# Four PSUM banks for the scan during the 5x5 convolution of images 1 to 3

## The chip, the cores and the metric

The kernel runs on one core of one Trainium2 chip. The metric is the device time of one execution in microseconds, a median over runs. The core has five engines with a queue each: TensorE (PE, with its weight loads as PEld), VectorE (DVE), ScalarE (ACT), GpSimd (POOL) and SyncE (SP, which issues DMAs here). PSUM, where matmuls put their results, is used in eight banks of 128 x 512 fp32.

## The reference, cut to what matters

Four layers, each pre-normed and residual, on `x` of 4 images, 128 channels, 64 x 64 pixels, all fp32:

```python
x = x + attention(_gn(x))          # 4096 pixels attend to each other, per image
x = x + conv5x5(_gn(x))            # radial 128 -> 128 kernel, padding 2
x = x + scan_layer(_gn(x))         # Wx, two directions of a state-space scan, Wp
x = x + conv3x3(_gn(x))            # main_w, main_b; the offset branch selects out or out
```

`_gn` is a group norm with 32 groups of four channels. In the scan layer each direction has 64 channels and 64 states: for every channel and state the recurrence is `h[t] = exp(delta[t] * A) * h[t-1] + delta[t] * x[t] * B[t]` over the 4096 pixels, and `y[t]` is the sum over states of `h[t] * C[t]`, plus `D * x[t]`.

## The kernel before

**The scan and its ticks.** `scan_core` cuts one image's scan into 256 ticks (`TICKS`), 1024 in all. A tick is a chunk of 1024 pixels (`CH`), a direction, a group of four states (`q`, 16 of them) and one of two channel groups of 32 (`g`), so that 128 partitions hold 32 channels by four states. Its steps lie on different engines:

- `drive(i)` (L1250): GpSimd, `db = dx * B`, 128 x 1024, three buffers.
- `decay(i, h)` (L1235): ScalarE, `da = exp(a * delta)`, written to PSUM. With two banks free for a tick it is done in two halves of 512, from three one-bank buffers of the pool `s2`. With the pool `wide` it is one instruction of 1024 over two banks, from two two-bank buffers.
- `recur(i)` (L1255): VectorE, the scan itself (L1263), in halves or whole, and where `to_pool(i)` is false also the product with C (L1266).
- `weigh(i)` (L1281): GpSimd, the product with C where `to_pool(i)` is true (L1284).
- `keep(i)` (L1271): ScalarE, saves the last column for the next chunk (L1279).
- `collect(i)` (L1286): TensorE, sums states into the bank `y` by small matmuls (L1304), for four ticks at a time. The tiles `hc` between the products and these matmuls have eight buffers.

`to_pool` (L1197) gives GpSimd two of every five products as a rule, three of five while `"operands"` is in `ready`, one of five while `"drives"` is, and one of three in the last image.

**The rest of the work.** Everything else is written as generators that yield the estimated cost of what they issued. `images()` (L1481) does image 0 up to its scan operands, then for each further image attention, `conv_pairs` (the 5x5 convolution), `scan_prep` and `scan_operands`, and at last the back parts (output projection and 3x3 convolution). `program` (L1376) walks the ticks: in each half of a tick it adds half of `pace` to a credit (2.8 us a tick, 1.5 for the last image) and takes steps from `images()` until the credit is used. So while the scan of image b-1 runs, attention and convolution of image b are laid between its ticks, and the order on every engine is that of the issue. `before(b)` (L1537) draws all steps that are missing until the first operands of image b are ready, four ticks ahead of its first tick.

**Around the change.** At the end of `attention` (L663) `settle` issues the last block and puts `(b, "attended")` in `ready`. `conv_pairs` (L828) begins with memsets on GpSimd, the group norm (13 small VectorE instructions, and two on GpSimd, L381 and L382), and four `normalise` pieces on ScalarE (L387). Then it does four chunks of matmuls (L962), which use the banks `s`, `a` and `z`. For images 1 to 3 it is `lean`: the first sum `q` is added by one more matmul (L989), and VectorE adds the result to the image (L930) with a running sum for the next norm. After the last addition `(b, "convolved")` is set and `scan_prep` (L1001) issues memsets and the next group norm. Attention uses the bank `s2` for scores; `scan_operands` uses it as one of three for the matmuls of L1044 and L1079. `conv_pairs` doesn't.

**The banks.** Four banks (`s`, `a`, `z`, `y`) are always there. The other four are the pool `s2` (one bank of that tag, three of `da`) or the pool `wide` (two `da` tiles of two banks). `widen` (L1503) swaps to `wide` once, when all operands of the last image are issued. At a swap the loop does `recur(i)` and `keep(i)` first, closes the old pool, opens the new, and only then issues the next `decay`.

Of the kernel before, what the change touches and what calls it, by code (L numbers as in the profile page):

```python
# [29 lines left out]
PSUM = bass.MemoryType.PSUM  # L30
# [15 lines left out]
PRODUCT, HOP, SLOT, PACE, ENDPACE, AHEAD = 0.86, 1.7, 0.7, 2.8, 1.5, 4  # L46
# [6 lines left out]
def conv_preact_kernel(  # L53
# [17 lines left out]
    B, C, H, W = x.shape  # L71
# [19 lines left out]
    pools, ready = {}, set()  # L91
# [345 lines left out]
    def attention(b, xs, xn, v, st, safe, loads):  # L437
# [141 lines left out]
        def settle(blk):  # L579
            raw, pb = state.pop(blk)  # L580
            cut = bass.ts(blk, MM)
            nc.vector.tensor_tensor(pb, raw, pb, ALU.mult)
            nc.vector.scalar_tensor_tensor(  # L583
                xs[:, cut], pb, bv_c, xs[:, cut], ALU.add, ALU.add, accum_out=st.sum(blk)
            )
            st.squares(blk, xs[:, cut], xs[:, 0:1])
# [75 lines left out]
        yield PRODUCT  # L662
        settle(blk)  # L663
        ready.add((b, "attended"))


    def conv(b, xs, tag, st, weights, k, finish, name, residual=False):
# [147 lines left out]
    def more_weights(cw, to):  # L815

        w = [cw[:, n * 5 : (n + 1) * 5, :] for n in range(3)]
        half, dif = to[:, 0], to[:, 1]
        nc.vector.tensor_tensor(half, w[0], w[2], ALU.add)
        yield HOP  # L820
        nc.vector.tensor_scalar(half, half, 0.5, None, ALU.mult)
        yield HOP
        nc.vector.scalar_tensor_tensor(dif, w[1], -0.5, half, ALU.mult, ALU.add)
        yield HOP
        nc.vector.scalar_tensor_tensor(half, w[1], 0.5, half, ALU.mult, ALU.add)
        yield HOP

    def conv_pairs(b, xs, tag, st, st2, lean):  # L828
# [36 lines left out]
        wide = pools.get("fill") if not lean else None  # L865
# [70 lines left out]
        for c in range(L // CH):  # L936
# [20 lines left out]
            for n, (acc, parts) in enumerate(accs):  # L957
# [13 lines left out]
                if n == 0:  # L971
                    qs = pools["bg"].tile([P, MM], F32, tag="w", bufs=4, name=f"q_{b}_{c}")

                    def done(acc=acc, qs=qs, c=c):
                        nc.scalar.copy(qs, acc)
                        for y in range(0 if lean else 2):
                            nc.gpsimd.tensor_tensor(
                                chunk(xs, c, y), chunk(xs, c, y), flat(qs), ALU.add
                            )
# [14 lines left out]
        yield HOP  # L994
        done()
        ready.add((b, "convolved"))

# [185 lines left out]
    def scan_core(mats4, ynds, before, widen, result):  # L1185


        ticks = [
            (b, c, d, q, g) for b in range(B)
            for c in range(NCH) for d in range(2) for q in range(NQ) for g in range(KG)  # L1190
        ]
# [5 lines left out]
        def to_pool(i):  # L1197


            if i not in pooled:  # L1200
                n = i % 5
                pooled[i] = (
                    i % 3 == 2 if ticks[i][0] + 1 == B
                    else n == 1 if "drives" in ready
                    else n % 2 == 0 if "operands" in ready else n % 2 == 1
                )
            return pooled[i]
# [73 lines left out]
        def weigh(i):  # L1281
            b, c, d, q, g = ticks[i]
            if to_pool(i):
                nc.gpsimd.tensor_tensor(hcs[i], hcs[i], rows["c", b, c, d, q], ALU.mult)  # L1284
# [49 lines left out]
        n = len(ticks)  # L1334

        def do(step, i, *args):
            if 0 <= i < n:
                step(i, *args)

        for i in range(-AHEAD, n + 4):  # L1340
            if (i + AHEAD) % TICKS == 0 and i + AHEAD < n:
                before((i + AHEAD) // TICKS)
            do(drive, i + 2)
            do(keep, i - 1)
            late = widen is not None and i + 1 < n and ticks[i][0] == B - 1 and widen()
            if not late:
                do(decay, i + 1, 0)
            do(recur, i)
            if late:
                do(keep, i)  # L1350
                late()
                widen = None
                do(decay, i + 1, 0)
            do(weigh, i - 1)
            do(collect, i - 3)
            yield i
            do(decay, i + 1, 1)
            do(load, i + AHEAD)
            yield i
# [16 lines left out]
    def program(safe):  # L1376
# [65 lines left out]
        def end(b, pieces):  # L1442

            xs, st, yt = ends[b]
            yield from scan_end(b, xs, st, yt, pieces)
# [35 lines left out]
        def images():  # L1481
            begun = yield from start(0)
            for b in range(B):
                begun = yield from front(b, *begun)
            for a in range(B - 1):
                yield from stage(a, range(NM), "scan")
                yield from end(a, range(NM))
                yield from back(a)
            for pieces, done in ((inner, "inner"), (last, "last")):
                yield from stage(B - 1, pieces, done)  # L1490
                yield from end(B - 1, pieces)
            yield from stage(B - 1, range(PER), "lower")
            ready.add((B - 1, "staged"))

        with ExitStack() as es, tc.manual_schedule():
            if safe:
                pools["big"] = es.enter_context(tc.tile_pool(name="big_safe", bufs=1))
                pools["bg"] = es.enter_context(tc.tile_pool(name="bg_safe", bufs=2))
            banks = ExitStack()
            pools["s2"] = banks.enter_context(tc.tile_pool(name=f"narrow{safe}", bufs=1, space=PSUM))  # L1500
            pools.pop("wide", None)

            def widen():  # L1503

                def swap():
                    banks.close()
                    pools["wide"] = es.enter_context(
                        tc.tile_pool(name=f"wide{safe}", bufs=1, space=PSUM)
                    )
                    del pools["s2"]  # L1510

                return swap if (B - 1, "all") in ready else None

            work = images()
            if not safe:
                with tc.tile_pool(name="fill", bufs=2) as pools["fill"]:
                    while not (0, "begun") in ready:
                        next(work)
                    more = [
                        pools["fill"].tile([P, NTAP, C], F32, tag="taps", bufs=1, name="taps"),  # L1520
                        pools["fill"].tile([P, 2, 5, C], F32, tag="more", bufs=1, name="more"),
                    ]

                    with tc.tile_pool(name="tables", bufs=1) as tmp:
                        for _ in chain(scan_constants(), build_conv_weights(tmp, more[0]), more_weights(*more)):
                            for _ in range(4):
                                next(work)
                    while (0, "convolved") not in ready:
                        next(work)
                del pools["fill"]  # L1530
                setup.close()
            pools["rep"] = es.enter_context(tc.tile_pool(name=f"rep{safe}", bufs=3))
            pools["rows"] = es.enter_context(tc.tile_pool(name=f"rows{safe}", bufs=3))
            pools["hc"] = es.enter_context(tc.tile_pool(name=f"hc{safe}", bufs=8))
            pace = PACE

            def before(b):  # L1537

                nonlocal pace
                while (b, "operands", 0) not in ready:  # L1540
                    next(work)
                if b + 1 == B:
                    pace = ENDPACE

            def result():

                while (B - 1, "staged") not in ready:
                    next(work)
                return ends[B - 1][2]

            credit = 0.0
            for i in scan_core(mats4, ynds, before, widen, result):
                if i % TICKS == 6 and i > TICKS:
                    ready.add((i // TICKS - 1, "scan"))
                if i == B * TICKS - TICKS // NCH + 6:
                    ready.update({(B - 1, "inner"), (B - 1, "lower")})
                if i == B * TICKS - TICKS // NCH // 2 + 6:
                    ready.add((B - 1, "last"))
                credit = min(credit + pace / 2, pace)
                while credit > 0:  # L1560
                    credit -= next(work, pace)
            for _ in work:
                pass
            for _ in chain(end(B - 1, range(PER)), back(B - 1)):
                pass

    program(False)
    lower.close()

# [12 lines left out]
    with tc.If(again > 0):  # L1582
        program(True)
# [59 lines left out]
```

## Time and profile before

| | |
|---|---|
| time, median of 3 runs | 4448.21 us (4447.31 to 4449.51) |
| the profiled execution | 4449.83 us |
| its span, first to last instruction | 4448.0 us |
| TensorE busy | 3922.3 us, 88% |
| VectorE busy | 3722.6 us, 84% |
| GpSimd busy | 3637.1 us, 82% |
| ScalarE busy | 2398.0 us, 54% |
| granted TensorE clock, mean | 0.936 |
| first tick of images 0, 1, 2, 3 | 695.3, 1648.7, 2595.6, 3537.1 us |
| 5x5 convolution of images 1, 2, 3 on TensorE | from 1384.9, 2328.2, 3272.7 to 1560.5, 2506.3, 3448.2 us |
| first unparted tick | tick 772, at 3568.7 us |

Shares over the whole span mix stages: image 0 runs without a scan, three images run with all engines shared, and the last image's scan has the back parts beside it. Busy times of TensorE are from modelled ends, so starts are the better measure there. A group line gives line, engine, operation, output and inputs with shapes, count, busy us, mean ns, and after the bar the idle time of the engine just before and what ended it. A line of the timeline gives start, length, engine, line, operation and, in brackets, idle time before it with its releaser. A line by stretch gives for each engine its busy us and instructions, then the granted clock, the share of the DMA engines and GB/s.

### The profile page before, as it was taken

Reading aid. Unit: us, or ns where it says so; the run is one execution under the profiler, and the core shown is the slowest. Engines: PE = TensorE matmul, PEld = TensorE weight load, DVE = VectorE, ACT = ScalarE, POOL = GpSimd, SP = SyncE. Lnnn points to the kernel's source line nnn. Section 1 sums busy time; section 2 is a strip of 40 time slices with the busy share of each in tenths; the row PEclk is TensorE's granted clock in tenths of the full one; section 3 lists DMA queues with packets and bytes.
Section 4 is the critical chain, followed back from the end, with each engine's and each line's share of the span. In section 5 each row is a group of like instructions: output and inputs, shape, how many; then the busy total and the mean of one; then the engine's idle time right before and its main releaser. Section 6 shows DMA issues by size and latency. Waiting matters only on the chain. (4 is left out here: it accounts for less than half of the span.)

```text
span 4448.0 us, 43613 instructions
## 1 busy us (share of the span) xinstructions
PE 3922.3 (88%) x13480; PEld 1492.0 (34%) x13480; DVE 3722.6 (84%) x3703; ACT 2398.0 (54%) x4425; POOL 3637.1 (82%) x1728
## 2 busy tenths in 40 slices
PE   8999997999999979999999889999999657576666
PEld 4444433333333323333333333333333112121222
DVE  4722217999999978999999889999999899999995
ACT  3333226666665476666664576666654754444532
POOL 3433307999999978999999889999999899999995
PEclk9999999999999989999999989999999869787887
DMA  1000016545545565455545565455445666656562
GB/s 64 21 1 1 0 55 230 182 163 178 178 173 177 178 228 195 173 178 173 182 167 173 205 228 178 166 178 179 169 178 178 225 217 208 229 199 232 189 228 78
DMA packets 213171, 726.10 MB, mean 163 GB/s; under 512 B 25152, under 2 KB 26432, under 8 KB 212672
## 3 DMA queue, kind: packets, MB, share of 16 engines
q1 hardware_dynamic: 211328, 722.49, 46.0%
q8 instruction: 108, 1.77, 0.2%
q14 instruction: 135, 1.11, 0.1%
q10 hardware_dynamic: 1600, 0.73, 0.1%
HBM read 653.98 MB, written 69.14 MB: 163 GB/s over the span
## 5 line engine op out<-in xcount | busy, mean ns | idle before, releaser
L1253 POOL TENSOR_TENSOR db<-dx,br 128x1024 f32<-128x1024 f32 x1024 | 2398.3, 2365 | 219.5 <-DMA dx<-dxd 59.5
L1246 ACT ACTIVATE da<-de,a_neg 128x512 f32<-128x512 f32 (+1 forms) x1796 | 1343.9, 751 | 741.7 <-DVE da L1263 435.5
L482 PE MATMUL sc<-r,x 128*128 128x512 f32 x2048 | 1080.8, 610 | 11.1 <-ACT last L1279 5.2
L494 PE MATMUL acc<-exchange,v 128*128 128x512 f32 x2048 | 1050.2, 595 | 2.2
L1284 POOL TENSOR_TENSOR hc<-hc,cr 128x1024 f32<-128x1024 f32 x401 | 947.9, 2364 | 17.8 <-ACT last L1279 15.3
L1266 DVE TENSOR_TENSOR hc<-da,cr 128x512 f32<-128x512 f32 (+1 forms) x1078 | 835.5, 775 | 66.8 <-DVE da L1263 0.5
L488 ACT ACTIVATE exchange<-sc 128x512 f32<-128x512 f32 x1024 | 603.2, 589 | 513.6 <-PE sc L482 508.3
L1304 PE MATMUL y<-hc,sel 128*32 128x512 f32 x4096 | 606.4, 647 | 261.6 <-POOL hc L1284 248.7
L1263 DVE TENSOR_TENSOR_SCAN da<-da,last,db 128x512 f32<-128x512 f32 (+1 forms) x464 | 728.3, 1570 | 17.2 <-POOL db L1253 14.7
L1263 DVE TENSOR_TENSOR_SCAN da<-da,da,db 128x512 f32<-128x512 f32 x455 | 585.5, 1287 | 14.9 <-ACT da L1246 14.4
L482 PEld LDWEIGHTS sc<-r,x 128*128 128x128 f32 x2048 | 363.1, 190 | 579.7 <-issue 383.8
L494 PEld LDWEIGHTS acc<-exchange,v 128*128 128x128 f32 x2048 | 387.2, 190 | 499.5 <-issue 479.3
L1263 DVE TENSOR_TENSOR_SCAN hc<-da,last,db 128x512 f32<-128x512 f32 (+1 forms) x304 | 455.7, 1499 | 2.3 <-POOL db L1253 0.7
L1263 DVE TENSOR_TENSOR_SCAN hc<-da,hc,db 128x512 f32<-128x512 f32 x317 | 406.7, 1283 | 43.5 <-ACT da L1246 13.8
L536 POOL TENSOR_TENSOR sidep<-sidep,exchange 128x512 f32<-128x512 f32 x120 | 170.9, 1424 | 273.3 <-ACT exchange L488 271.0
L1304 PEld LDWEIGHTS y<-hc,sel 128*32 128x32 f32 x4096 | 114.6, 112 | 692.4 <-POOL hc L1284 342.1
L536 DVE TENSOR_TENSOR sided<-sided,exchange 128x512 f32<-128x512 f32 x120 | 95.9, 799 | 221.5 <-ACT exchange L488 220.1
L1263 DVE TENSOR_TENSOR_SCAN da<-da,db 128x512 f32<-128x512 f32 (+1 forms) x159 | 235.8, 1483 | 11.3 <-ACT da L1246 7.3
L696 PE MATMUL pcm<-xpm,cs 128*128 128x512 f32 x432 | 211.7, 639 | 35.8 <-ACT xpm L387 35.8
L516 PE MATMUL zp<-exchange,ones 128*32 128x512 f32 x1536 | 205.6, 600 | 11.6 <-DVE xs L583 11.6
L962 PE MATMUL pe<-df,exchange 128*128 128x512 f32 x480 | 213.7, 595 | 0.0
L1279 ACT COPY last<-da 128x1 f32<-128x1 f32 x474 | 73.9, 156 | 254.3 <-DVE hc L1266 251.8
(241 smaller groups left out, 2851.1 us busy)
## 6 DMA issues: line engine op xcount, KB each, us to landing
br<-bm SPq DMA_DIRECT2D x512, 512.0 KB, 5.2
cr<-cm SPq DMA_DIRECT2D x512, 512.0 KB, 3.9
de<-dd SPq DMA_DIRECT2D x64, 512.0 KB, 4.9
dx<-dxd SPq DMA_DIRECT2D x64, 512.0 KB, 6.4
x<-in_x_dram SPq DMA_DIRECT2D x16, 512.0 KB, 5.2
xs<-in_x_dram SPq DMA_DIRECT2D x16, 512.0 KB, 6.1
xsd<-xs SPq DMA_DIRECT2D x16, 512.0 KB, 6.5
xcd<-xc SPq DMA_DIRECT2D x16, 512.0 KB, 3.0
```

The lines of the kernel that those rows point to most:

```text
L482: nc.tensor.matmul(sc, xn[:, bass.ts(j, P)], rq[blk], start=True, stop=True)
L488: nc.scalar.activation(pt, sc, AF.Exp)
L494: nc.tensor.matmul(acc[blk], v[:, j, :], ring[:, u % NRING, :], start=j == 0, stop=j == NJT - 1)
L536: eng.tensor_tensor(s, s, ring[:, u % NRING, :], ALU.add)
L696: nc.tensor.matmul(acc.rearrange("p (r w) -> p r w", w=W), weights[:, t, :], xp[:, y : y + RPM, dx : dx + W], start=t == 0, stop=t == k * ...
L962: nc.tensor.matmul(flat(acc), matrix(w, dx), view(r, dx), start=k == 1, stop=k == total and (n == 0 or not lean),)
L1246: nc.scalar.activation(da, rep["de", b, c, d, g][:, bass.ts(h, size)], AF.Exp, scale=a_neg[:, at(i)])
L1253: nc.gpsimd.tensor_tensor(dbs[i], rep["dx", b, c, d, g], rows["b", b, c, d, q], ALU.mult)
L1263: nc.vector.tensor_tensor_scan(h, da, db[:, cut], before, ALU.mult, ALU.add)
L1266: nc.vector.tensor_tensor(hc[:, cut], h, rows["c", b, c, d, q][:, cut], ALU.mult)
L1284: nc.gpsimd.tensor_tensor(hcs[i], hcs[i], rows["c", b, c, d, q], ALU.mult)
L1304: nc.tensor.matmul(y[r : r + SG, :], sel, hcs[first + gg][:, bass.ts(h, MM)], start=q == back, stop=False, tile_position=(0, r), skip_grou ...
```

## The change

A flag `"convolving"` is set when attention of an image after the first is issued, and taken away when its 5x5 convolution is. `widen` now asks for four banks while the flag is set, as well as after the last image's operands, and for two otherwise; it can swap in both directions and in any tick, and the pools are opened anew under numbered names. After the convolution `conv_pairs` yields `HOP` until the scan has gone back, since the preparation needs the bank `s2`. `to_pool` follows the banks and no longer the image: one of three products on GpSimd while the ticks are unparted, and the rule of five else.

```diff
@@ attention
         settle(blk)
         ready.add((b, "attended"))
+        if b > 0:
+            ready.add("convolving")
@@ conv_pairs
         done()
         ready.add((b, "convolved"))
+        ready.discard("convolving")
+        while b > 0 and "wide" in pools:
+            yield HOP
@@ scan_core, to_pool
-                    i % 3 == 2 if ticks[i][0] + 1 == B
+                    i % 3 == 2 if "wide" in pools
@@ scan_core, the loop over ticks
-            late = widen is not None and i + 1 < n and ticks[i][0] == B - 1 and widen()
+            late = i + 1 < n and i >= 0 and widen()
...
                 late()
-                widen = None
@@ program
-            banks = ExitStack()
+            banks = es.enter_context(ExitStack())
...
+            turns = []
+
             def widen():
+                wide = (B - 1, "all") in ready or "convolving" in ready
 
                 def swap():
+                    old, new = ("s2", "wide") if wide else ("wide", "s2")
                     banks.close()
-                    pools["wide"] = es.enter_context(
-                        tc.tile_pool(name=f"wide{safe}", bufs=1, space=PSUM)
+                    del pools[old]
+                    turns.append(new)
+                    pools[new] = banks.enter_context(
+                        tc.tile_pool(name=f"{new}{safe}_{len(turns)}", bufs=1, space=PSUM)
                     )
-                    del pools["s2"]
-
-                return swap if (B - 1, "all") in ready else None
+
+                return swap if wide != ("wide" in pools) else None
@@ program, result
-                    next(work)
+                    next(work, None)
```

## The prediction

> **What bounds the kernel now.** I read the slices and groups of the page first, then busy time by stretch, then the waits inside the middle of the first covered convolution (1400 to 1550 us), then the order of time around its two ends. The groups, with shapes kept apart, price both kinds of tick (count, busy us, mean ns, idle before):
>
> ```profile
> L1253 POOL TENSOR_TENSOR db<-dx,br 128x1024 f32<-128x1024 f32 x1024 | 2398.3, 2365 | 219.5 <-DMA dx<-dxd 59.5 <-DVE hc L1263 56.8 <-DVE da L1263 25.7
> L1284 POOL TENSOR_TENSOR hc<-hc,cr 128x1024 f32<-128x1024 f32 x401 | 947.9, 2364 | 17.8 <-ACT last L1279 15.3 <-DVE hc L1263 2.2
> L1266 DVE TENSOR_TENSOR hc<-da,cr 128x512 f32<-128x512 f32 x910 | 629.7, 692 | 50.7
> L1263 DVE TENSOR_TENSOR_SCAN hc<-da,hc,db 128x512 f32<-128x512 f32 x317 | 406.7, 1283 | 43.5 <-ACT da L1246 13.8 <-DVE hc L1263 0.5
> ...
> L1263 DVE TENSOR_TENSOR_SCAN da<-da,last,db 128x1024 f32<-128x1024 f32 x128 | 299.8, 2342 | 6.0 <-POOL db L1253 5.8
> ...
> L1266 DVE TENSOR_TENSOR hc<-da,cr 128x1024 f32<-128x1024 f32 x168 | 205.8, 1225 | 16.2 <-DVE da L1263 0.5
> ```
>
> A two-bank tick costs VectorE two scans (about 1.28 us each) and, where GpSimd doesn't take the product, two products of 0.69: starts in the trace are 2.58 us apart with the product on GpSimd and 3.85 without. With two of five ticks given to GpSimd the mean is (2 x 2.58 + 3 x 3.85) / 5 = 3.34. GpSimd pays 2.365 for every drive and 2.364 for two of five products: 3.31. An unparted tick starts 2.26 or 3.57 us after the one before in the final stretch; with one of three on GpSimd that is (2.26 + 2 x 3.57) / 3 = 3.13, and GpSimd has 2.365 + 2.364 / 3 = 3.15.
>
> So over the some 52 ticks of one convolution the change takes 52 x 0.21 = 10.9 us from VectorE and 52 x 0.16 = 8.2 us from GpSimd, three times. Whether that is time depends on TensorE. Busy time by stretch (the middles of the three convolutions, then a stretch of attention; columns PE, PEld, DVE, ACT, POOL):
>
> ```profile
> 1400.00:1550.00 150.00, 150.00 (x475) 59.32 (x474) 144.77 (x152) 68.33 (x108) 147.20 (x66) 1.00 0.53 179
> 2340.00:2500.00 160.00, 159.76 (x507) 62.26 (x505) 151.97 (x159) 72.46 (x114) 155.97 (x71) 1.00 0.49 170
> 3290.00:3440.00 150.00, 150.00 (x477) 59.12 (x476) 144.96 (x153) 68.09 (x108) 146.75 (x66) 1.00 0.49 175
> 900.00:1200.00 300.00, 294.68 (x1128) 110.09 (x1130) 285.03 (x293) 192.50 (x398) 276.53 (x120) 1.00 0.51 176
> ```
>
> Three engines are full at once. Modelled ends could make TensorE look full, so I checked starts: matmuls of L962 follow each other every 0.43 us without a hole, the waits view of TensorE in 1400 to 1550 is empty, and 475 records come out as 303 x 0.43 + 44 groups of four parallel y matmuls x 0.43 = 149 us. TensorE runs behind its program, on work that the other engines don't feed, and catches up: in that stretch it does 303 / 2 x 0.86 / 43 ticks = 3.0 units of convolution a tick where PACE issues 2.8. Its order is fixed by PACE, so a faster VectorE can't end the convolution on TensorE earlier.
>
> What a faster VectorE can move is what follows. TensorE, then VectorE, at the end of the first covered convolution:
>
> ```profile
> 1557.51 1.92 PE L1304 MATMUL y<-hc,sel 128*32 128x512 f32 x16
> 1559.36 1.12 PE L989 MATMUL pe<-q,ident 128*128 128x512 f32 x2
> 1573.44 2.74 PE L1044 MATMUL pt<-xn,wtap 128*64 128x512 f32 x4 [12.96 <-ACT xn L387]
> ```
>
> ```profile
> 1564.52 1.28 DVE L1263 TENSOR_TENSOR_SCAN hc<-da,last,db 128x512 f32<-128x512 f32 x1
> 1565.90 1.28 DVE L1263 TENSOR_TENSOR_SCAN hc<-da,hc,db 128x512 f32<-128x512 f32 x1
> 1567.10 0.67 DVE L930 SCALAR_TENSOR_TENSOR xs<-pe,xs 128x512 f32<-128x512 f32 x1
> ```
>
> TensorE is done at 1560.5; VectorE gets to the last addition at 1567.1, because three ticks are queued ahead of it. Then group norm, then 12.96 us of idle TensorE end. The same lag is 7.0 us in the second (2506.3 to 2513.3) and 6.9 in the third (3448.2 to 3455.1): 6.6 + 7.0 + 6.9 = 20.5 us.
>
> [...]
>
> **The change part by part.** I stepped the costs that the generators yield against PACE, tick by tick; for the kernel before this gives 772 as the first four-bank tick, as in the trace. For the changed one: four banks from tick 192 to 244, 446 to 498, 702 to 754, and 775 to the end: 53 x 3 + 249 = 408 unparted scans where there are 252.
>
> *Can VectorE catch up?* Eight hc buffers hold it: tick 240 can't begin before the y matmuls of tick 232, at 1545.1 to 1546.5. From there ticks 240 to 243 take 3 x 3.57 + 2.26 = 13.0, and one addition 0.7: 1560.2, just in time for the last matmul. Over the whole stretch VectorE needs 52 x 3.13 + 5 of additions + about 1.4 of swap = 169 us from 1385.6: 1555, so it does reach the hold. GpSimd takes 17 products where it took 21, so four less x 2.36 = 9.5 us: it ends at 1558 where it ended at 1567.7. The last addition thus comes at 1560.6 to 1561.6. I take 1 us short per image: -20.5 + 3 = -17.5.
>
> *Swap to four banks.* The swap in the trace costs VectorE 1.43 us: the new exponential (1.12 us) waits for the scan before it. Queued behind it on ScalarE are the keep copy and the second normalise piece, which TensorE needs 10 x 0.43 = 4.3 us after its first matmul; by my count it arrives 2.8 to 4.2 us after. The first piece is ahead of the swap in all three. VectorE's hole is hidden by the hc hold. Nothing on the path, 0 to +1 us each if the piece is late; I put +0.5 in all.
>
> *Swap back and the wait loop.* One tick (2.26 or 3.57 us) now lies between the last addition and the group norm; the 1.4 us hole falls under the 13 small VectorE instructions of the norm (2.9 us). That tick isn't lost in the second and third image: the final stretch, bound by VectorE and GpSimd, has one tick less of 3.13, so +0.4 each. In the first image preparation has to be done by tick 252, so there a tick is missing in it instead. A tick beside preparation costs about 1.5 us ((75.3 us from its first matmul to tick 256, less the 56 it takes alone for the first image) / 11), so of 3.6 about 2.1 stay. Sum +2.9.
>
> *The rest.* The final swap comes three ticks later: 3 x 0.2 = +0.6. The final image's ticks before it follow the five-tick rule and no longer one in three: two products move at most, 0 +- 2. No DMA is added or moved past a queue; tickwise loads stay with their ticks.
>
> Sum: -17.5 + 0.5 + 2.9 + 0.6 = -13.5. The profiled execution had a span of 4448.0 and a time of 4449.8; the median is 4448.2. Taking the sum from the median: 4434.7, put at 4435.
>
> **The rivals.**
> A, the above, chance 0.57: 4427 to 4442 us.
> B, TensorE isn't the bound: its full look is a queue that follows the ticks, and all that VectorE saves shows. 3 x 10.9 = 33 less the same 4: 4419 (4413 to 4426). For it: VectorE shows 96% and no waits to speak of. Against it: no hole and no wait on TensorE. Chance 0.13.
> C, the lag isn't made up: GpSimd, at 98%, holds the drives, or the second piece comes late in each image, and only some 2 us an image remain before the swap's costs: 3 x 2 - 4 = 2 gained, 4446 (4441 to 4452). Chance 0.18.
> D, slower: the convolution is bound by TensorE, so unparted ticks there bring nothing, and the swaps' price is paid on the path: six times 1.43 us and three waits of 3.57 us that the final stretch doesn't give back, 8.6 + 10.7 = 19 us: 4467. It decides if the last addition doesn't come nearer than some 6 us to the last matmul. Against it: the hc hold leaves room for two ticks, and total ticks are fixed. Chance 0.12.
> That the change does nothing is excluded by the code, since the flag is set in three images.
>
> **How the numbers follow.** The range of A alone is 4427 to 4442. To leave out no more than two in ten (D, and the low half of B) it goes from 4418 to 4451. A measurement of this kernel can tell some 0.2% (8.9 us) from no change; A lies beyond that but for a tenth of it, B wholly, C within, D beyond on the other side: faster 0.65, same 0.23, slower 0.12.
>
> **What would show it.** Right: about 408 unparted scans; TensorE still without holes and waits in the middle of each convolution, VectorE down from 145 to about 138 of 150 us and waiting for y matmuls; the last addition within 1.5 us of the last L989; the TensorE gap after it 9 to 11 us where it was 12.96, 11.56 and 13.26. Wrong: holes on TensorE (B), an addition still 5 us late (C, D), or a second piece that TensorE waits for at a convolution's start.

## The result, and the profile after

The changed kernel takes 4429.16 us (median of 6 runs, 4425.80 to 4431.28) where the kernel before takes 4447.83 (4447.27 to 4449.51). The ratio is 0.9961 with a 95% interval of 0.9951 to 0.9971, that is 13 to 22 us faster; 13.2 were forecast. A later comparison gave 0.9966 (0.9954 to 0.9978). The profiled execution took 4425.80 us, with a span of 4424.0.

The granted TensorE clock isn't the cause: its mean over the runs of the kernel before is 0.938, and 0.938 too over those of `e9_early_shift` below, which has the whole gain. Counted in the trace, the unparted ticks are 192 to 244, 446 to 498, 702 to 754 and 775 to the end, 408 in all, as worked out. The groups with shapes kept apart (line, engine, operation, shapes, count, busy us and mean ns, idle before) show that prices didn't change; only counts did:

```profile
L1258 POOL TENSOR_TENSOR db<-dx,br 128x1024 f32<-128x1024 f32 x1024 | 2398.1, 2365 | 223.8 <-DMA dx<-dxd 55.6 <-DVE hc L1268 42.5 <-DMA br<-bm 31.9
L1289 POOL TENSOR_TENSOR hc<-hc,cr 128x1024 f32<-128x1024 f32 x386 | 913.0, 2365 | 22.5 <-ACT last L1284 19.7 <-DVE hc L1268 1.6 <-DVE da L1268 1.1
L1268 DVE TENSOR_TENSOR_SCAN da<-da,last,db 128x1024 f32<-128x1024 f32 x235 | 550.7, 2344 | 17.8 <-ACT da L1251 8.6 <-POOL db L1258 7.7 <-ACT last L1284 1.2
L1271 DVE TENSOR_TENSOR hc<-da,cr 128x1024 f32<-128x1024 f32 x273 | 334.4, 1225 | 23.4 <-DVE da L1268 0.5 <-issue 0.4
```

Busy time in the middles of the three convolutions (columns PE, PEld, DVE, ACT, POOL, then clock, DMA share, GB/s):

```profile
1400.00:1550.00 150.00, 150.00 (x475) 59.20 (x474) 141.46 (x89) 57.79 (x65) 142.75 (x65) 1.00 0.53 183
2335.00:2485.00 150.00, 150.00 (x477) 59.04 (x476) 139.70 (x88) 57.22 (x65) 143.20 (x65) 1.00 0.48 176
3278.00:3428.00 150.00, 150.00 (x476) 58.79 (x474) 139.93 (x88) 58.03 (x66) 142.19 (x65) 1.00 0.51 179
```

TensorE does the same 475 to 477 matmuls in the same 150 us, still without a hole; VectorE and GpSimd are the ones that got room. From first to last L964 or L991 a convolution takes 175.5, 175.5 and 175.2 us (175.6, 178.1 and 175.5 before). The gain lies behind it. TensorE, then VectorE, at the end of image 1's convolution:

```profile
1557.61 1.12 PE L991 MATMUL pe<-q,ident 128*128 128x512 f32 x2
1569.19 2.73 PE L1049 MATMUL pt<-xn,wtap 128*64 128x512 f32 x4 [10.46 <-ACT xn L387]
```

```profile
1556.71 2.33 DVE L1268 TENSOR_TENSOR_SCAN da<-da,last,db 128x1024 f32<-128x1024 f32 x1
1559.13 1.23 DVE L1271 TENSOR_TENSOR hc<-da,cr 128x1024 f32<-128x1024 f32 x1
1560.27 0.68 DVE L932 SCALAR_TENSOR_TENSOR xs<-pe,xs 128x512 f32<-128x512 f32 x1
1560.88 2.35 DVE L1268 TENSOR_TENSOR_SCAN da<-da,last,db 128x1024 f32<-128x1024 f32 x1
```

The last addition comes 1.5 us after the last matmul, where it came 6.6. The last line is the tick that the wait puts ahead of the norm: the gap on TensorE shrinks less than the lag, from 12.96 to 10.46 us.

For all kernels run, worked out from their traces: "lag" is from the end of the last L989/L991 matmul to the start of the last addition; "gaps" is the sum over the three images of the time from that end to the first matmul of preparation (`pt`); "back" is the tick that VectorE is in when the first output projection of the back stages (`po` from `xt`) starts; "preparation" from image 1's first pt matmul to the first scores of image 2; "to 775" from the first scores of image 1 to tick 775, which leaves out differences at the start; "stretch" from tick 775 to tick 1023.

| kernel | lag, images 1, 2, 3 | gaps | back | preparation | to 775 | stretch | ratio (95%) |
|---|---|---|---|---|---|---|---|
| before | 6.6, 7.0, 6.9 | 39.6 | 781 | 102.8 | 2845.8 | 796.6 | 1 |
| changed | 1.5, 3.5, 3.5 | 35.5 | 784 | 95.2 | 2829.5 | 793.4 | 0.9961 (0.9951 to 0.9971) |
| changed, run again | 1.5, 3.5, 3.5 | 35.5 | 784 | 94.6 | 2830.9 | 793.4 | 0.9966 (0.9954 to 0.9978) |
| e1_ratio | 7.2, 8.2, 8.7 | 43.2 | 781 | 101.9 | 2849.7 | 800.9 | 1.0024 (1.0014 to 1.0035) |
| e2_fifths | 0.7, 4.5, 2.3 | 41.2 | 784 | 94.7 | 2837.6 | 795.0 | 0.9990 (0.9981 to 0.9998) |
| e3_wait | 6.6, 8.0, 7.0 | 49.2 | 784 | 94.8 | 2846.5 | 796.4 | 1.0003 (0.9995 to 1.0012) |
| e4_early | 3.5, 5.1, 5.1 | 32.6 | 781 | 102.5 | 2832.7 | 804.5 | 0.9993 (0.9984 to 1.0001) |
| e5_late | 2.3, 3.5, 3.5 | 36.2 | 784 | 95.2 | 2835.8 | 796.6 | 0.9965 (0.9952 to 0.9979) |
| e6_first | 4.6, 8.1, 5.4 | 37.2 | 781 | 102.4 | 2841.3 | 800.4 | 0.9997 (0.9988 to 1.0005) |
| e7_fifths_act | 0.6, 4.5, 2.2 | 40.2 | 784 | 94.7 | 2839.5 | 793.4 | 0.9974 (0.9963 to 0.9984) |
| e8_after_act | 1.5, 3.5, 3.5 | 37.5 | 784 | 94.8 | 2835.8 | 791.1 | 0.9966 (0.9952 to 0.9979) |
| e9_early_shift | 3.5, 5.1, 5.1 | 32.6 | 784 | 102.0 | 2830.6 | 793.7 | 0.9963 (0.9949 to 0.9976) |
| e10_before_shift | 6.6, 7.6, 6.9 | 40.2 | 784 | 101.4 | 2840.7 | 794.5 | 0.9987 (0.9980 to 0.9995) |
| e12_wait2 | 1.5, 3.5, 3.5 | 40.3 | 784 | 99.2 | 2828.9 | 796.4 | 0.9961 (0.9948 to 0.9975) |

One profile's "to 775" has a spread of some 5 us: the kernel before and `e10_before_shift` do the same until tick 770, and differ by 5.1 at 775. So ratios decide below, and the columns show where. In the kernels without a wait after the convolution the gaps come to the lags and 19 us; the wait adds 8 to 9 us in the changed kernel, `e3_wait` and `e5_late`.

### The profile page after: what moved, and what is told of

The parts are those of the page before. It is cut to its first block, busy times and chain, and to the rows that moved or that the text cites. A ratio compares the mean times of both kernels' runs of the same rounds, so it can differ in the third digit from the quotient of the medians.

```text
span 4424.0 us, 43050 instructions
## 1 busy us (share of the span) xinstructions
PE 3917.4 (89%) x13480; PEld 1485.9 (34%) x13480; DVE 3698.5 (84%) x3472; ACT 2358.3 (53%) x4269; POOL 3602.1 (81%) x1713
## 5 line engine op out<-in xcount | busy, mean ns | idle before, releaser
L1251 ACT ACTIVATE da<-de,a_neg 128x512 f32<-128x512 f32 (+1 forms) x1640 | 1302.4, 797 | 740.6 <-DVE da L1268 300.5
L1289 POOL TENSOR_TENSOR hc<-hc,cr 128x1024 f32<-128x1024 f32 x386 | 913.0, 2365 | 22.5 <-ACT last L1284 19.7
L1268 DVE TENSOR_TENSOR_SCAN da<-da,last,db 128x512 f32<-128x512 f32 (+1 forms) x480 | 863.1, 1798 | 24.3 <-POOL db L1258 12.1
L1268 DVE TENSOR_TENSOR_SCAN hc<-da,last,db 128x512 f32<-128x512 f32 (+1 forms) x288 | 490.9, 1704 | 6.5 <-ACT da L1251 5.2
L1268 DVE TENSOR_TENSOR_SCAN da<-da,da,db 128x512 f32<-128x512 f32 x365 | 469.7, 1287 | 6.2 <-ACT da L1251 5.9
L1268 DVE TENSOR_TENSOR_SCAN hc<-da,hc,db 128x512 f32<-128x512 f32 x251 | 322.0, 1283 | 35.6 <-ACT da L1251 11.8
L964 PE MATMUL pe<-df,exchange 128*128 128x512 f32 x480 | 214.2, 595 | 0.0
```

Of the source, the lines that this page charges most:

```text
L964: nc.tensor.matmul(flat(acc), matrix(w, dx), view(r, dx), start=k == 1, stop=k == total and (n == 0 or not lean),)
L1251: nc.scalar.activation(da, rep["de", b, c, d, g][:, bass.ts(h, size)], AF.Exp, scale=a_neg[:, at(i)])
L1268: nc.vector.tensor_tensor_scan(h, da, db[:, cut], before, ALU.mult, ALU.add)
```

## The experiments

**Which queue ends the convolution?** First the change's ratio alone, on two banks:

```diff
-                    i % 3 == 2 if ticks[i][0] + 1 == B
+                    i % 3 == 2 if ticks[i][0] + 1 == B or "convolving" in ready
```

> The kernel before, with one product of three on GpSimd during the convolutions of images 1 to 3 and nothing else: two banks, halves, no swap, no wait. Queue theory (what counts is how many us of VectorE ticks stand ahead of the last addition when TensorE ends the convolution): a tick costs VectorE (2.58 + 2 x 3.85) / 3 = 3.43 us instead of 3.34, 52 x 0.09 = 4.7 us more lag an image, so the last addition comes 11 to 12 us after the last matmul and the time goes up by about 3 x 4.5 = 13 us, to 4461 us (4453 to 4466). Rival, GpSimd (at 98% it holds the drives, and the change helped by taking four products of 2.36 us from it): GpSimd is relieved as in the changed kernel, and the time goes down by 8 to 18 us, to 4430 to 4440 us.

Measured: 1.0024, about 11 us slower. GpSimd was relieved as in the changed kernel, VectorE was loaded, the lag rose to 7.2, 8.2 and 8.7 us. That is far less than the 11 to 12 us expected: of the 11 us, 3.5 are in the gaps, image 1's convolution took 181.7 us instead of 175.6, and the final stretch is 4 us longer. The sign speaks for the queue theory, its size doesn't. Less work on GpSimd alone is no gain; VectorE's queue counts.

Then the other half: four banks and unparted ticks, with the old share of GpSimd.

```diff
-                    i % 3 == 2 if "wide" in pools
+                    i % 3 == 2 if "wide" in pools and (B - 1, "all") in ready
```

> The changed kernel with two of five products on GpSimd during the convolutions, as before; four banks, swaps and wait stay. Queue theory: a tick costs VectorE (2 x 2.26 + 3 x 3.57) / 5 = 3.05 us, less than with one of three (3.13), so it reaches the hold of the hc buffers as well and the last addition follows the last matmul within 4 us; the time stays within 5 us of the changed kernel, 4424 to 4434 us. GpSimd rival: GpSimd's load per tick is 3.31 us as before the change, so the lag stays at 6 to 7 us and the gain falls by more than half, to 4440 us or more.

Measured: 0.9990, some 4 us gained of 17. The queue theory was about right on the lag (0.7, 4.5 and 2.3 us) and wrong on the time; the GpSimd rival was right that over half of the gain goes, and wrong on the lag. TensorE's gap in image 1 is nevertheless 13.1 us, and VectorE's timeline behind the addition shows the loss; GpSimd's beside it:

```profile
1566.41 0.16 DVE L338 TENSOR_REDUCE gn_sums<-su_s 128x2 f32<-128x16 f32 x1
1566.60 3.76 DVE L339 TENSOR_SCALAR gcols<-gn_sums 128x2 f32<-128x2 f32 x1
1570.39 0.16 DVE L340 TENSOR_TENSOR aw_s<-gcols,aw_s 128x1 f32<-128x1 f32 x1
```

```profile
1563.32 4.64 POOL L1258 TENSOR_TENSOR db<-dx,br 128x1024 f32<-128x1024 f32 x2
1567.93 2.33 POOL L1289 TENSOR_TENSOR hc<-hc,cr 128x1024 f32<-128x1024 f32 x1
1570.21 0.09 POOL L1012 MEMSET xn<- 128x3 f32 x1
1570.24 0.09 POOL L1013 MEMSET xn<- 128x3 f32 x1
```

Scaling two numbers took 3.76 us (2.65 and 2.48 in the other two images, 3.08, 1.20 and 1.41 in the final stretch, 0.17 in the other six norms), and ended when GpSimd's queue paused: here the norm doesn't get past GpSimd's backlog, even on VectorE. So with this code the change needs both parts, shorter ticks for VectorE and fewer products for GpSimd.

To see whether that one instruction is the cause it was moved to ScalarE, in the kernel with fifths and in the changed one:

```diff
-            nc.vector.tensor_scalar(gcols[:, :, 0], total, 1.0 / L, None, ALU.mult)
+            nc.scalar.activation(gcols[:, :, 0], total, AF.Identity, scale=1.0 / L)
```

> The changed kernel with two of five products on GpSimd in the convolutions (as in the run with fifths), and the scaling by 1/L in the norms (L339) moved from VectorE to ScalarE. In the run with fifths that one instruction took 3.76, 2.65 and 2.48 us on VectorE in the three norms after the convolution, where it takes 0.17 with GpSimd idle, and ended when GpSimd came to rest. [...] the stall goes, 2 to 3 us an image, and 1 to 2 us in each of three norms of the final stretch; 8 to 12 us faster than with fifths, ratio to before 0.9963 to 0.9972. Rival (GpSimd's own queue, with the power in the norm behind it, is what lasts): after the stall is gone GpSimd is as late as before, and no more than 4 us is gained, ratio 0.998 to 0.999.

> The changed kernel with the same move of L339 to ScalarE. In its profile the instruction took 0.23, 0.59 and 0.17 us after the convolutions, so nothing is gained there; in the final stretch it took 2.35, 1.09 and 1.13 us. [...] about 4 us faster than the changed kernel, if VectorE is on the path of the final stretch in these places. Rival (GpSimd's queue lasts longest there): no difference within 2 us.

Measured: 0.9974 and 0.9966. The first lies between its two expectations. It is better than with fifths alone, but the intervals meet at 0.9981 to 0.9984, and its gaps on TensorE (12.8, 14.3 and 13.1 us) are only 0.3 us shorter; its interval meets that of the changed kernel too, so what the fewer products are worth isn't settled by it. The stall had moved to the next instruction, in VectorE's timeline of `e7_fifths_act`:

```profile
1562.73 0.16 DVE L338 TENSOR_REDUCE gn_sums<-su_s 128x2 f32<-128x16 f32 x1
1563.76 2.83 DVE L340 TENSOR_TENSOR aw_s<-gcols,aw_s 128x1 f32<-128x1 f32 x1 [0.87 <-ACT gcols L339]
1566.63 0.22 DVE L341 SCALAR_TENSOR_TENSOR gcols<-aw_s,gcols 128x1 f32<-128x1 f32 x1
```

GpSimd came to rest at 1566.65 there, and L340 ended at 1566.59; with fifths alone the two times were 1570.33 and 1570.36, for L339. The `tensor_reduce` just before (L338) took 0.16 us in both, with GpSimd at work. So the stall went with GpSimd's queue and not with L339 alone; what causes it isn't shown. In the changed kernel L339 took 0.23, 0.59 and 0.17 us after the convolutions, so there was nothing to gain. The 4 us expected from the final stretch didn't show either (0.9966 beside 0.9966 for the changed kernel).

**Does it matter when VectorE saves?** The flag set at the third of four chunks, and the flag taken away there:

```diff
+            if b > 0 and c == 2:
+                ready.add("convolving")        # e5_late, instead of after attention
...
+            if c == 2:
+                ready.discard("convolving")    # e6_first
```

> The changed kernel with the flag set only at the third of four chunks of the convolution, so that some 26 of its 53 unparted ticks are left, the later ones. Queue theory with the hold of eight hc buffers: VectorE is at the hold when the convolution begins and falls behind by 0.13 us a tick on two banks, so the later half alone makes up what the whole does: last addition 3 to 4 us after the last matmul (6.5 to 7 before, 1.5 to 3.4 in the changed kernel), and the changed kernel's gain nearly whole, ratio to before 0.9961 to 0.9972. Rival (saved VectorE time counts wherever it is saved): half the gain, 0.998 to 0.9987.

> The changed kernel with the flag taken away at the third chunk: the earlier half of the unparted ticks, and no wait at the end. Queue theory: VectorE reaches the hold early, can't go on, and falls back by 3 to 4 us on the two-bank ticks that follow; last addition 4 to 5.5 us after the last matmul, a third of the gain to tick 775 (5 us of 16). The back stages begin at tick 770 as in the kernel before, so the final stretch takes 797 to 804 us: ratio to before 0.998 to 1.000. Rival (saved time counts wherever it is saved): half the gain, 8 us to tick 775, and the same final stretch.

Measured: 0.9965 for the later half, 0.9997 for the earlier, both as the queue theory expected. The two kernels differ in more than the half: `e5_late` keeps the wait after the convolution and begins the back stages later (784 in the table), `e6_first` does neither. Each has a kernel on two banks that is like it in both. Against `e3_wait`, below, the later half gains 17 us (10 to 24); against the kernel before, the earlier half gains 1 us (-2 to 5). Half the unparted ticks give the whole gain or next to none, by their place. The waits of VectorE in image 2's convolution (2335 to 2485 us; total, times, longest) show why, in the changed kernel and then in `e6_first`:

```profile
DVE xs L932 <- PE pe L991: 6.4, 4, 2.2
```

```profile
DVE xs L932 <- PE pe L993: 5.6, 2, 4.5
```

In this image, what VectorE saves early it loses again waiting for TensorE. But it waits in its own additions, which stand in its queue between ticks, and not for hc buffers as I had it. In `e5_late` this wait doesn't appear in the same window, and the lags are those of the changed kernel.

**What do the wait and the swap back cost?** The wait alone in the kernel before, and the changed kernel with the flag taken away some two ticks before the end of the convolution:

```diff
+            ready.discard("waiting")           # e3_wait, head of each tick
...
+        if b > 0:
+            ready.add("waiting")
+        while "waiting" in ready:
+            yield HOP
```

```diff
+                        if (c, n, k) == (L // CH - 1, len(accs) - 1, 12):
+                            ready.discard("convolving")    # e4_early
```

> The kernel before, with the wait alone: after the convolution of images 1 to 3 it yields until the scan has begun its next tick; two banks throughout, no swap. Queue theory: one tick of 2.58 to 3.85 us goes between last addition and group norm, is given back by the final stretch in two images and in part by preparation in the first; +2 to +4 us, 4450 to 4452 us. Rival (the wait is paid in full on the path): 3 x 3.6 = +11 us, 4459 us.

> The changed kernel, with the flag taken away some two ticks earlier, before the last matmuls of the last chunk, so that the scan is back on two banks when the convolution is issued and nothing has to wait. Queue theory: two ticks of four banks less an image (0.4 us more lag), and the tick between addition and group norm is gone: 2 to 4 us faster than the changed kernel, 4425 to 4427 us. Rival (the wait is paid in full): 10 us faster, 4419 us. If the swap back costs on the path when it lies ahead of the last addition instead of under the group norm: 3 x 1.4 us of that is lost, 4429 to 4431 us.

Measured: 1.0003 for the wait (-2 to +5 us), as expected or less. But this isn't the wait alone: each wait holds the other work back by a tick, so that the back stages begin later as well (784 where the kernel before has 781). `e10_before_shift`, below, begins them as late and doesn't wait. Against it the wait costs 7 us (2 to 12), and the gaps are 9.0 us longer. TensorE at the end of image 1's convolution, in `e3_wait` and in `e10_before_shift`:

```profile
1557.17 1.13 PE L989 MATMUL pe<-q,ident 128*128 128x512 f32 x2
1574.62 1.97 PE L1048 MATMUL pt<-xn,wtap 128*64 128x512 f32 x3 [16.33 <-ACT xn L387]
```

```profile
1559.20 1.13 PE L989 MATMUL pe<-q,ident 128*128 128x512 f32 x2
1573.28 2.74 PE L1044 MATMUL pt<-xn,wtap 128*64 128x512 f32 x4 [12.95 <-ACT xn L387]
```

The early swap back came out at 0.9993, far worse than each expectation. Its profile is as good as the changed kernel's to tick 775 (2832.7 against 2829.5 and 2830.9) and loses 11 us after it, in a part that the edit moves but doesn't alter: there, GpSimd's waits from 3580 to 4350 us in `e4_early`, and in the changed kernel:

```profile
POOL db L1260 <- DMA br<-bm: 15.4, 11, 4.9
```

```profile
POOL db L1258 <- DMA br<-bm: 5.2, 9, 1.0
```

Rows of B arrive late. By the count of costs the back stages are issued from tick 773 in the changed kernel and from 770 in `e4_early` and before; their first output projection starts in tick 784 and 781. Holding them until tick 774, in `e4_early` and in the kernel before, tests whether this is all:

```diff
+            while "tail" not in ready:         # ahead of the back stages
+                yield HOP
...
+                if i == (B - 1) * TICKS + 6:
+                    ready.add("tail")
```

> The early swap back (nothing waits after the convolution), with the back stages of images 0 to 2 held until tick 774, where they begin in the changed kernel, instead of 770. Placement theory: the early swap back was as good as the changed kernel to tick 775 (3562.0 against 3559.7 us) and lost 11 us in the final stretch alone, where GpSimd waited 15.4 us for rows by DMA and 5.2 in the changed kernel, because the back stages' loads fell on other ticks; with the shift the final stretch takes 793 to 797 us from tick 775, and the ratio to before is 0.996 to 0.9975. Rival (the early swap back itself is worse, by the scan's ticks that it doesn't get done under the norm): it stays at 0.9985 to 0.9995.

> The kernel before, with only the back stages held until tick 774 (770 before). Placement theory: the final stretch from tick 775 takes 793.5 instead of 796.6 us, since the loads of the back stages fall on other ticks; 2 to 5 us faster, ratio 0.9989 to 0.9996. Rival (holding is lost time, since the back work has to be done): 0 to 4 us slower.

Measured: 0.9963 and 0.9987. With the shift the early swap back has the final stretch of the changed kernel (793.7 us; the wait for rows is 7.7 us) and its time. So going back early doesn't beat waiting: it has no wait, but 5 us more lag. Where the back stages fall does make a difference: 13 us (6 to 20) between `e4_early` and `e9_early_shift`, and 0.13% (2 to 9 us) in the kernel before, with no other change. Why the stretch of `e4_early` is 8 us longer than that of the kernel before, where the back stages begin in the same tick, isn't shown.

> The changed kernel itself, beside the other kernels of this batch, as their measure. Its ratio to the kernel before was 0.9961; the same is expected here (0.995 to 0.997).

Measured: 0.9966, and 4429.97 us.

**What shortens image 1's preparation?** It takes about 95 us in kernels that wait after the convolution and 101 to 103 in those that don't. One more tick of waiting in image 1:

```diff
+        if b == 1:
+            ready.add("waiting")
+        while "waiting" in ready:
+            yield HOP
```

> The changed kernel with one more tick of waiting after the convolution of image 1 alone. In the run with the wait alone image 1's preparation (first pt matmul to the first scores of image 2) took 94.8 us and 102.9 in the kernel before, with one tick less beside it. If it is the number of ticks beside preparation: another 3 us less there against 3 us more ahead of it, 0 +- 2 us from the changed kernel. If a wait is paid: 3 us slower. If the 8 us came from where a tick's instructions fall in the queues: the preparation changes by several us either way, without order.

Measured: 0.9961. The preparation took 99.2 us, 4 to 5 more than with one tick of waiting, though a tick fewer lies beside it. So it isn't the number of ticks. The placement of ticks in the queues fits, but which instruction makes the 8 us remains open. They aren't the gain: from the first scores of image 1 to those of image 3 the changed kernel takes 1878.5 us, and `e4_early` and `e9_early_shift`, with the long preparation, 1878.2 and 1875.1.

No version is better than the changed kernel beyond its interval.

## Why the prediction was right or wrong, point by point

**Tick prices and counts: right.** The 408 unparted scans lie in the ticks named, at the means named.

**TensorE bounds the convolution: right.** Its length stayed at 175 to 176 us (image 2's went from 178.1 to 175.5), and rival B, where all that VectorE saves shows, is out: `e6_first` saves half of it for next to nothing.

**VectorE catches up: right in direction, mis-sized.** The lags fell from 20.5 to 8.5 us, so -12.0 stands where the sum has -17.5. The step that failed is the hold: I let eight hc buffers hold VectorE, and in image 2 it was held by additions queued behind each other. VectorE's last two there, and TensorE's last matmul:

```profile
2478.14 0.69 DVE L932 SCALAR_TENSOR_TENSOR xs<-pe,xs 128x512 f32<-128x512 f32 x1 [1.33 <-PE pe L991]
2497.41 0.67 DVE L932 SCALAR_TENSOR_TENSOR xs<-pe,xs 128x512 f32<-128x512 f32 x1
```

```profile
2492.91 1.02 PE L991 MATMUL pe<-q,ident 128*128 128x512 f32 x2
```

Six ticks lie between the two additions: 6 x 3.13 + 0.7 = 19.5 us of VectorE, while TensorE needs 15.8 to its end at 2493.9. No earlier saving can shorten that. Of the signs named, the addition within 1.5 us came true in image 1 alone, VectorE was busy for 140 to 141 us of 150 and not 138, and it didn't wait for y matmuls.

**GpSimd ends in time: right, and it matters.** With the old share the lag shrank and some 4 of 17 us were gained. Rival C had GpSimd as the limit, but by way of the drives; what stalled was a small VectorE instruction of the norm.

**Swap to four banks, +0.5: right within what can be seen.** Convolutions didn't get longer.

**Wait and swap back, +2.9: too small.** `e3_wait` measured +1.3 (-2 to +5), but with the back stages begun later; against `e10_before_shift`, alike in that, it is +7 (2 to 12). From the end of the convolution the gaps on TensorE fell by 2.5, 0.7 and 0.9 us only, since the waited tick lies in them. I took most of that tick to be given back later; the gaps grow by 9.0 us in `e3_wait`, and some 7 show in the time. Rival D, where nothing is gained against this, is out. The price of 1.5 us for a tick beside preparation was wrong twice: (75.3 - 56) / 11 is 1.75, and there is no fixed price, since image 1's preparation moved by 4 to 8 us with the placement.

**The rest, +0.6: wrong in sign.** I counted the later final swap as three dearer ticks and took the back work to be hidden wherever it began. Beginning it three ticks later is worth -5.8 us in the kernel before (-9 to -2). That it collides less with the scan's row loads fits: GpSimd's waits for rows of B and dx from 3580 to 4350 us fall from 19.7 to 13.6 us. It isn't shown, for in `e3_wait` they fall to 13.5 and the stretch stays at 796.4.

**The sum.** The wait's +1.3 already holds the later start of the back stages, so the terms as measured are -12.0 + 1.3 = -10.7, or -12.0 + 7.1 - 5.8 with the two apart, where the ratio has 17 us (13 to 22). Some 6 us have no term here; the intervals of the single terms are 4 to 5 us each way, so this may be noise or something not found. That -13.5 lay near the result was in part luck: the catch-up was overestimated, the wait was underestimated, and the placement was missed.

The mechanism is better shown than the sum, by kernels that are alike in the wait and in the start of the back stages. The times are differences of the ratios, times 4445 us:

| from, to | gaps on TensorE | time (95%) |
|---|---|---|
| e3_wait, changed | -13.7 | -19 (-25 to -13) |
| e3_wait, e5_late | -13.0 | -17 (-24 to -10) |
| e3_wait, e7_fifths_act | -9.0 | -13 (-19 to -7) |
| e3_wait, e2_fifths | -8.0 | -6 (-11 to 0) |
| e10_before_shift, e9_early_shift | -7.6 | -11 (-18 to -4) |
| before, e4_early | -7.0 | -3 (-7 to 0) |
| before, e6_first | -2.4 | -1 (-5 to 2) |
| before, e1_ratio | +3.5 | +11 (6 to 16) |

A shorter gap goes with a shorter time of about the same size; `e1_ratio` alone lies clearly off, and its first convolution and final stretch got longer as well. So what four banks gain lies for the most part between the end of the convolution on TensorE and the preparation, as forecast.

## What to carry to other kernels

Here TensorE was full (150 of 150 us in the middle of each convolution), and a saving on VectorE was worth about what it took from the queue ahead of TensorE's next work: in the later half of the stage it gained 17 us (10 to 24), in the earlier half 1 us (-2 to 5). So put such a saving late in the stage. Look at every queue that the stage's last result passes: here with VectorE's shortened and GpSimd's not, some 4 of 17 us were gained. A side effect that shifts a later stage by three ticks moved the time by 6 and 13 us here, beside a gain of 17, so test the shift alone, and compare an edit with a control that has the same shift.

## What the runs showed of the hardware

In `e2_fifths`, after image 1's convolution, a VectorE instruction on two numbers per partition (L339) took 3.76 us beside a busy GpSimd, where it took 0.17 in six of the kernel's twelve norms. It lasted past the end of a single GpSimd instruction (at 1567.9 us in the lines above) and ended at 1570.36, when GpSimd's queue paused (1570.33). The `tensor_reduce` just before it (L338) kept its 0.16 us. When L339 went to ScalarE (`e7_fifths_act`), VectorE's next instruction of the norm (L340) took 2.83 us where it had taken 0.16.
